# One-hot matrices for two pairs of edge tiles by one comparison, with its row of numbers in PSUM, in a graph network on one Trainium2 core

## The chip, the core and the metric

The kernel runs on one of the eight cores of a Trainium2 chip. A core has five engines that work side by side and wait for each other through semaphores: TensorE (PE in the profile, its weight loads PEld), VectorE (DVE), ScalarE (ACT), GpSimd (POOL) and SyncE (SP). SBUF is the working memory, 128 partitions wide; PSUM, in eight banks of 2 KB per partition, takes TensorE's results. The metric is the time of one execution in microseconds (us), as the device counts it; the median of three runs is compared.

## The reference

There are 6250 nodes with 256 features and 100000 edges, sorted by their destination, with 32 attributes and one of three types each. Three layers follow each other, and then the input is added and each node normalised:

```python
ew = edge_attr @ edge_w + edge_b
inv_cnt = [1.0 / max(segment_sum(type == i, dst), 1.0) for i in range(3)]
for l in range(3):
    msg = relu(x[src] * ew)
    out = zeros((n, 256))
    for i in range(3):
        h = segment_sum(msg * (type == i), dst) * inv_cnt[i]
        out = out + h @ weights[l, i]
    x = x + relu(out + x @ roots[l] + biases[l])
return layernorm(x_in + x)
```

All is fp32.

## The kernel before

The edges are cut into tiles of 128, two of which make a pair: 391 pairs, taken in a fixed order (`order`). Two pairs form a block `q`. A step (`it`) of the loop in `layer` stands for one pair, and code for pairs that lie ahead is issued in it, so that each engine's instructions stand in the order in which the loop writes them (`tc.manual_schedule`); nothing reorders them. Per step and in this order the loop

- gathers the source rows of the pair nine steps ahead, by two indirect DMAs from GpSimd (`gather_pair`, L1054) into a row tile `xs` for two pairs, of which there are eight (`rows`, `bufs=ROWS`); in the first layer from the input, later from `x_mid`, which the layer before wrote. The first three row tiles of the whole run lie in `x_root` instead;
- reduces the pair itself (`reduce`, L687 or L695): a matmul of its messages with the one-hot matrix of each of its tiles, 120 columns for 3 types x 40 nodes, summed over a span of pairs in a bank of `h_p`;
- multiplies edge attributes by `edge_w` for the pair five ahead (`make_ew`, L634), into `ew_p`, which ScalarE has filled with the bias (L621);
- weighs the block three ahead (`weigh`): VectorE multiplies `xs` by `ew_p` in place (L656), ScalarE takes the relu (L657);
- handles one root chunk of 128 nodes, about every six steps: `root_turn` transposes `x_all` on TensorE (L728), two steps later ScalarE copies that (L732), at the third step TensorE multiplies by `roots` (L736), and at the sixth VectorE adds the bias and keeps it in `x_root` (`root_keep`, L739);
- handles a node chunk whose edges are all in: TensorE multiplies the sums in `acc` by `weights` (`node_mul`, L754), VectorE scales and adds them to `x_root` (L785), adds the relu to `x_all` (L788), and SyncE writes the rows to `x_mid` (L791), or in the last layer VectorE normalises them (L806) and SyncE writes the output;
- builds the one-hot matrices of the block two ahead (`one_hot`, L669): four comparisons on VectorE, one for each tile, of the numbers 0 to 119 (`iota_w`, in SBUF) with the number `seg` of each edge. In the first layer ScalarE makes a bf16 copy (L673), from which edges are counted;
- adds a finished span's sums from `h_p` into the ring `acc` (`add`, L723).

At the start of layers 1 and 2 the first six pairs are gathered before the last node chunk is written; `complete` adds what that chunk brings, by matmuls (L649) and an add (L651).

PSUM is full: `ew_p` has four banks, `h_p` two, `o_p` and `r_p` one each. A tile of `r_p` holds a root chunk's transposes in its first half and its product in the second. `complete` and `node_mul` take turns between `o_p` and `r_p`: the second pair of a block in `complete`, and the second part of node chunks 0 and 1, go to `r_p`. Chunks 1 and 0 are the last two of a layer.

Of the kernel before, what the change touches and what calls it, by code (L numbers as in the profile page):

```python
# [8 lines left out]
F32 = mybir.dt.float32  # L9
BF = mybir.dt.bfloat16  # L10
I32 = mybir.dt.int32
AF = mybir.ActivationFunctionType
ALU = mybir.AluOpType
# [429 lines left out]
def ordered_path(ctx, tc, x, attr_laid, A, weights, roots, biases, edge_w, edge_b, out, src, src_i, seg, place_i, consts, x_root,  # L443
# [6 lines left out]
    nc = tc.nc  # L450
    P = 128
    N, D = x.shape
    E = src.shape[0]
    L, R = weights.shape[:2]
# [5 lines left out]
    DC = D // P  # L460
    WK = R * WIN
# [11 lines left out]
    ident, ones, iota_w = consts  # L473
# [14 lines left out]
    with tc.tile_pool(name="bias_s", bufs=1) as bias_s:  # L488
# [5 lines left out]
        part = bias_s.tile([P, D], BF, name="part")  # L494
# [10 lines left out]
    x_all = big.tile([P, NT, D], F32, name="x_all")  # L505
# [28 lines left out]
    wpool = ctx.enter_context(tc.tile_pool(name="wpool", bufs=1))  # L534
    o_pool = ctx.enter_context(tc.tile_pool(name="o_p", bufs=1, space=PSUM))
    r_pool = ctx.enter_context(tc.tile_pool(name="r_p", bufs=1, space=PSUM))

    at_groups = list(dict.fromkeys(u // GROUP for u in order))

# [47 lines left out]
    def layer(l, r_sb, b_sb, ats, early, pools):  # L587
# [11 lines left out]
        xs, ew_ps, ohs, h_ps, h_ss, o_ps, rs = {}, {}, {}, {}, {}, {}, {}  # L599
        x0s, mvs, oh_bs, t_ss, places = {}, {}, {}, {}, []  # L600
# [12 lines left out]
        def pairs_of(q):  # L613
            return range(min(2, U - 2 * q))
# [29 lines left out]
        def complete(q):  # L644
            for k in pairs_of(q):

                rest = (r_pool if k else o_pool).tile([P, 2, D], F32, name="r_p" if k else "o_p")
                for i in range(2):
                    nc.tensor.matmul(rest[:, i, :], came[:, 4 * q + 2 * k + i - 2 * order[0], :], x_all[:, 0, :],  # L649
                                     start=True, stop=True)  # L650
                nc.vector.tensor_add(xs[q][:, k], rest, xs[q][:, k])  # L651
# [13 lines left out]
        def one_hot(q):  # L665
            ohs[q] = edge.tile([P, 4, WK], F32, name="oh", bufs=3)
            n = 2 * len(pairs_of(q))
            for t in reversed(range(n)):
                nc.vector.tensor_scalar(ohs[q][:, t, :].rearrange("p (r w) -> p r w", r=R), iota_w[:, :, :WIN], seg[:, 4 * q + t:4 * q + t + 1], None,  # L669
                                        op0=ALU.is_equal)  # L670
            if l == 0:
                oh_bs[q] = edge.tile([P, 4, WK], BF, name="oh_b", bufs=3)
                nc.scalar.activation(oh_bs[q][:, :n], ohs[q][:, :n], AF.Copy)  # L673
# [49 lines left out]
            nc.vector.tensor_tensor(there, h_ps[span][:, :CH * WK].rearrange("p (c r w) -> p c r w", c=CH, r=R), there, op=ALU.add)  # L723

        def root_turn(c):
            rs[c] = r_pool.tile([P, 2, DC * P], F32, name="r_p")
            for d in range(DC):
                nc.tensor.transpose(rs[c][:, 0, d * P:(d + 1) * P], x_all[:, c, d * P:(d + 1) * P], ident)  # L728

        def root_turned(c):  # L730
            t_ss[c] = edge.tile([P, DC, P], F32, name="t_s", bufs=1)
            nc.scalar.activation(t_ss[c], rs[c][:, 0, :], AF.Copy)  # L732

        def root_mul(c):
            for d in range(DC):
                nc.tensor.matmul(rs[c][:, 1, :], t_ss[c][:, d, :], r_sb[:, d, :], start=(d == 0), stop=(d == DC - 1))  # L736

        def root_keep(c):
            nc.vector.tensor_add(x_root[:, at_root[c], :], rs[c][:, 1, :], b_sb)  # L739
            if l == L - 1:  # L740
                nc.vector.tensor_add(x_all[:, c, :], x_all[:, c, :], x0s[c])

        def parts_of(c):
            return ((0,), (1, 2)) if c else ((0,), (1,), (2,))

        def node_mul(c, part):

            n = min(P, N - c * P)
            slot = slot_of(c)
            o_p = o_ps[c, part] = (r_pool if part == 1 and c < 2 else o_pool).tile(  # L750
                [P, 2, D], F32, name="r_p" if part == 1 and c < 2 else "o_p")
            for j, r in enumerate(parts_of(c)[part]):
                for d in range(DC):
                    nc.tensor.matmul(o_p[:n, j, :], acc[:, d, r, slot:slot + n], w_sb[:, r * DC + d, :],  # L754
                                     start=(d == 0), stop=(d == DC - 1))
            if l == 0 and part == 0:
                for r in range(R):
                    nc.tensor.transpose(o_p[:n, 1, r:r + 1], acc[0:1, DC, r, slot:slot + n], ident[0:1, 0:1])

        def slot_of(c):  # L760
            return c % (RING // P) * P if c > 1 else ASIDE + c * P
# [57 lines left out]
        at_root = {c: (j + 2 * FIRST) % ROOTS for j, c in enumerate(turns_of)}  # L819
# [8 lines left out]
        for it in range(-11, max(starts) + 8):  # L828
            def pair(k):
                return order[it + k] if 0 <= it + k < U else None  # L830
# [28 lines left out]
            if pair(3) is not None and first_of(it + 3, 2):  # L859
                if l > 0 and it + 3 < FIRST:  # L860
                    complete(pair(3) // 2)
                if pair(3) // 2 != order[-1] // 2:
                    weigh(pair(3) // 2)

            if pair(3) is not None and pair(3) // 2 == order[-1] // 2:
                k = pair(3) % 2
# [6 lines left out]
            if it - 6 in root_at:  # L873
                root_keep(root_at[it - 6])
            if it in root_at:
                root_turn(root_at[it])
            if it - 2 in root_at:
                root_turned(root_at[it - 2])
            if it - 3 in root_at:
                root_mul(root_at[it - 3])  # L880
# [13 lines left out]
            if it in node_at:  # L894
                node_mul(node_at[it], 0)
            if it - 2 in node_at:
                node_mul(node_at[it - 2], 1)
                if node_at[it - 2] == 0:
                    node_mul(0, 2)
# [4 lines left out]
            if pair(2) is not None and first_of(it + 2, 2) and pair(2) // 2 != order[-1] // 2:  # L904
                one_hot(pair(2) // 2)
            if pair(3) is not None and first_of(it + 3, 2) and pair(3) // 2 == order[-1] // 2:
                one_hot(pair(3) // 2)
# [14 lines left out]
WIN = 40  # L922
# [137 lines left out]
def kernel(ctx, tc, x, src, dst, edge_attr, edge_type, weights, roots, biases, edge_w,  # L1060
# [110 lines left out]
    with tc.If(unordered == 0):  # L1171
        ordered_path(tc, x, attr_laid, edge_attr.shape[1], weights, roots, biases, edge_w, edge_b, out, src, src_i, seg, place_i,
                     (ident, ones, iota_w), x_root, first_rows, node_i)
# [51 lines left out]
```

## Time and profile before

| | us |
|---|---|
| median of three runs | 2961.4 (2960.73 to 2961.57) |
| the profiled execution | 2962.46 |
| its span, first to last instruction | 2960.2 |
| GpSimd busy / idle before its gathers | 2228.8 / 715.8 |
| VectorE busy | 1998.2 |
| four comparisons of a block, all 2346 | 622.9 |

The profile page gives for each engine the time in which it was busy with instructions, groups of instructions by line with the mean duration of one and the idle time before them, and the waits with what ended them. [...] Timeline rows read: start, duration, engine, line, operation, output <- inputs with partitions x elements, count, and in brackets the idle time before and what released it. Rows by windows give a stretch, its length, then for each engine the busy time and the number of instructions.

### The profile page before, as it was taken

To read this page: it belongs to the slowest core of one execution; us is meant where nothing else is said; L and a number is where in the kernel's file an instruction comes from. 1 tells how busy PE (TensorE), PEld (TensorE's weight loads), DVE (VectorE), ACT (ScalarE), POOL (GpSimd) and SP (SyncE) were. 2 spreads that over 40 slices of the span, in tenths; PEclk is the share of its full clock that TensorE was granted. 3 is DMA by queue.
4 is the path that set the end of the run, shared out by engine and by line. 5 is a ranking of instruction groups with operands and counts; after the bars stand their busy time and mean duration, and the time that the engine had idled before them with its cause. 6 is when DMAs were issued, how large, how long until landed. Compare 5 with 4: busy or idle time off the path is not lost. (4 is left out here: it accounts for less than half of the span.)

```text
span 2960.2 us, 43407 instructions
## 1 busy us (share of the span) xinstructions
PE 2591.9 (88%) x13712; PEld 1782.6 (60%) x13712; DVE 1998.2 (68%) x4910; ACT 1503.8 (51%) x1911; POOL 2228.8 (75%) x2355
## 2 busy tenths in 40 slices
PE   5999999999998878888889998778888888999876
PEld 2666677677765545556666666454555666666644
DVE  6666677778775555566767776545666777888864
ACT  4666656556565444454444444435444444444443
POOL 7777777777777777777777777777777777777776
PEclk9999999999999999999999999889999999999998
DMA  5444444444444444444444444444444444444443
GB/s 168 151 143 136 148 124 125 127 130 130 127 134 128 132 116 120 129 122 124 127 125 130 130 132 129 136 132 125 126 133 133 135 133 132 139 137 137 129 125 97
DMA packets 173705, 387.39 MB, mean 131 GB/s; under 512 B 43594, under 2 KB 79068, under 8 KB 173468
## 3 DMA queue, kind: packets, MB, share of 16 engines
q0 software_dynamic: 112608, 307.65, 36.4%
q1 hardware_dynamic: 53280, 68.50, 7.2%
q10 hardware_dynamic: 7580, 8.37, 1.0%
q8 instruction: 113, 1.85, 0.3%
q14 instruction: 124, 1.02, 0.1%
HBM read 364.89 MB, written 19.46 MB: 130 GB/s over the span
## 5 line engine op out<-in xcount | busy, mean ns | idle before, releaser
L1054 POOL DMA_INDIRECT xs<-x_mid,src_r x1540 | 1460.5, 948 | 469.1 <-issue 363.4
L657 ACT ACTIVATE xs<-xs 128x1024 f32<-128x1024 f32 (+1 forms) x585 | 615.7, 1053 | 1301.0 <-DVE xs L656 1296.5
L656 DVE TENSOR_TENSOR xs<-ew_p,xs 128x1024 f32<-128x1024 f32 (+1 forms) x585 | 711.4, 1216 | 676.7 <-DMA xs<-x_mid,src_r 429.8
L1054 POOL DMA_INDIRECT xs<-in_x_dram,src_io x770 | 732.0, 951 | 234.6 <-issue 192.3
L695 PEld LDWEIGHTS h_p<-oh,xs 128*128 128x128 f32 x5160 | 669.7, 196 | 251.9 <-issue 123.8
L695 PE MATMUL h_p<-oh,xs 128*128 128x120 f32 x5160 | 734.3, 287 | 86.4 <-issue 34.5
L634 PE MATMUL ew_p<-ew_sb,at 64*128 64x512 f32 x2346 | 687.6, 662 | 95.8 <-ACT ew_p L621 92.3
L669 DVE TENSOR_SCALAR oh<-iota_w,seg_o 128x120 f32<-128x120 f32 x2346 | 622.9, 327 | 0.0
L687 PE MATMUL h_p<-xs,oh 128*120 128x256 f32 x2088 | 570.9, 407 | 22.9 <-issue 7.8
L621 ACT ACTIVATE ew_p<-seed 128x1024 f32<-128x1024 f32 x582 | 588.9, 1012 | 0.0
L754 PE MATMUL o_p<-w_sb,acc 128*128 128x256 f32 (+1 forms) x1728 | 440.7, 391 | 28.2 <-DVE x_root L785 24.2
L687 PEld LDWEIGHTS h_p<-xs,oh 128*120 128x120 f32 x2088 | 363.1, 191 | 162.8 <-issue 48.1
L723 DVE TENSOR_TENSOR acc<-h_p,acc 128x240 f32 (+1 forms) x732 | 323.7, 442 | 173.2 <-PE o_p L754 69.6
L754 PEld LDWEIGHTS o_p<-w_sb,acc 128*128 128x128 f32 (+1 forms) x1728 | 309.3, 191 | 152.0 <-DVE x_root L785 62.7
L634 PEld LDWEIGHTS ew_p<-ew_sb,at 64*128 64x128 f32 x2346 | 181.9, 189 | 224.9 <-ACT ew_p L621 121.1
L785 DVE SCALAR_TENSOR_TENSOR x_root<-o_p,inv,x_root 128x256 f32<-128x256 f32 (+1 forms) x432 | 207.0, 479 | 28.3 <-PE o_p L754 21.6
L736 PE MATMUL r_p<-r_sb,t_s 128*128 128x256 f32 x588 | 160.1, 395 | 26.1 <-ACT t_s L732 25.8
L771 ACT ACTIVATE acc<-zero_o 128x768 f32<-128x768 f32 (+1 forms) x150 | 140.2, 934 | 15.3 <-PE o_p L754 14.7
L673 ACT ACTIVATE oh_b<-oh 128x480 bf16<-128x480 f32 x196 | 116.3, 594 | 56.1 <-DVE oh L669 55.2
L728 PEld LDWEIGHTS r_p<-ident_o,x_all 128*128 128x128 f32 x294 | 30.9, 144 | 169.0 <-DVE x_root L739 116.7
L736 PEld LDWEIGHTS r_p<-r_sb,t_s 128*128 128x128 f32 x588 | 103.0, 192 | 47.6 <-ACT t_s L732 36.4
L728 PE MATMUL r_p<-ident_o,x_all 128*128 128x128 f32 x294 | 65.4, 305 | 69.3 <-DVE x_root L739 69.1
(110 smaller groups left out, 940.8 us busy)
## 6 DMA issues: line engine op xcount, KB each, us to landing
at<-in_attr_laid_dram SPq DMA_DIRECT2D x147, 256.0 KB
xs<-x_mid,src_r POOLq DMA_INDIRECT x1540, 2.8
xs<-in_x_dram,src_io POOLq DMA_INDIRECT x770, 2.8
x_mid<-x_all SPq DMA_DIRECT2D x96, 128.0 KB
x_all<-in_x_dram ACTq DMA_DIRECT2D x8, 768.0 KB
x<-in_x_dram SPq DMA_DIRECT2D x48, 128.0 KB
out_dram<-x_all SPq DMA_DIRECT2D x48, 128.0 KB
w_sb<-in_L_gnn_weights_dram SPq DMA_DIRECT2D x3, 768.0 KB
```

What stands on the lines that cost most here:

```text
L621: nc.scalar.activation(ew_ps[q][:, :n], seed[:, None, :, :].to_broadcast([P, n, 2, D]), AF.Copy)
L634: nc.tensor.matmul(ew_ps[q][:, k].rearrange("p i d -> p (i d)"), at[half, :], ew_sb[half].rearrange("p i d -> p (i d)"), start=False, stop ...
L656: nc.vector.tensor_mul(there, ew_ps[q][:, pairs.start:pairs.stop], there)
L657: nc.scalar.activation(there, there, AF.Relu)
L669: nc.vector.tensor_scalar(ohs[q][:, t, :].rearrange("p (r w) -> p r w", r=R), iota_w[:, :, :WIN], seg[:, 4 * q + t:4 * q + t + 1], None, o ...
L687: nc.tensor.matmul(h_p[:WK, :D], ohs[u // 2][:, t, :], xs[u // 2][:, u % 2, i, :], start=(i == 0 and first), stop=(i == 1 and closes(u)), ...
L695: nc.tensor.matmul(h_p[:, d * WK:(d + 1) * WK], xs[u // 2][:, u % 2, i, d * P:(d + 1) * P] if d < DC else full_ones, (ohs if d < DC else o ...
L723: nc.vector.tensor_tensor(there, h_ps[span][:, :CH * WK].rearrange("p (c r w) -> p c r w", c=CH, r=R), there, op=ALU.add)
L736: nc.tensor.matmul(rs[c][:, 1, :], t_ss[c][:, d, :], r_sb[:, d, :], start=(d == 0), stop=(d == DC - 1))
L754: nc.tensor.matmul(o_p[:n, j, :], acc[:, d, r, slot:slot + n], w_sb[:, r * DC + d, :], start=(d == 0), stop=(d == DC - 1))
L785: nc.vector.scalar_tensor_tensor(root, o_p[:n, j, :], inv[:n, c, r:r + 1], root, op0=ALU.mult, op1=ALU.add)
L1054: nc.gpsimd.indirect_dma_start(out=xs[:, u % 2, i, :], out_offset=None, in_=x_rows[:, :], in_offset=bass.IndirectOffsetOnAxis(ap=src_i[:, ...
```

## The change

One bank of `r_p` is held by one tile for the whole run. Its second half takes a copy of the numbers 0 to 119, written once (L539 of the changed kernel). The first half serves a root chunk's transposes and then, over them, its product. `one_hot` becomes one `tensor_tensor` per block (L671): the row of numbers from PSUM, repeated for each tile, against `seg`, repeated over 120 columns. `complete` uses `o_p` for both its pairs, and of the node chunks only chunk 0's second part still uses `r_p`'s half bank.

```diff
--- before.py
+++ after.py
@@ -534,6 +534,9 @@
     wpool = ctx.enter_context(tc.tile_pool(name="wpool", bufs=1))
     o_pool = ctx.enter_context(tc.tile_pool(name="o_p", bufs=1, space=PSUM))
     r_pool = ctx.enter_context(tc.tile_pool(name="r_p", bufs=1, space=PSUM))
+    r_bank = r_pool.tile([P, 4 * P], F32, name="r_p")
+    r_p, places_p = r_bank[:, :D], r_bank[:, None, D:D + WK]
+    nc.vector.tensor_copy(r_bank[:, D:D + WK].rearrange("p (r w) -> p r w", r=R), iota_w[:, :, :WIN])
 
     at_groups = list(dict.fromkeys(u // GROUP for u in order))
 
@@ -644,7 +647,7 @@
         def complete(q):
             for k in pairs_of(q):
 
-                rest = (r_pool if k else o_pool).tile([P, 2, D], F32, name="r_p" if k else "o_p")
+                rest = o_pool.tile([P, 2, D], F32, name="o_p")
                 for i in range(2):
                     nc.tensor.matmul(rest[:, i, :], came[:, 4 * q + 2 * k + i - 2 * order[0], :], x_all[:, 0, :],
                                      start=True, stop=True)
@@ -665,9 +668,8 @@
         def one_hot(q):
             ohs[q] = edge.tile([P, 4, WK], F32, name="oh", bufs=3)
             n = 2 * len(pairs_of(q))
-            for t in reversed(range(n)):
-                nc.vector.tensor_scalar(ohs[q][:, t, :].rearrange("p (r w) -> p r w", r=R), iota_w[:, :, :WIN], seg[:, 4 * q + t:4 * q + t + 1], None,
-                                        op0=ALU.is_equal)
+            nc.vector.tensor_tensor(ohs[q][:, :n], places_p.to_broadcast([P, n, WK]),
+                                    seg[:, 4 * q:4 * q + n, None].to_broadcast([P, n, WK]), op=ALU.is_equal)
             if l == 0:
                 oh_bs[q] = edge.tile([P, 4, WK], BF, name="oh_b", bufs=3)
                 nc.scalar.activation(oh_bs[q][:, :n], ohs[q][:, :n], AF.Copy)
@@ -723,20 +725,19 @@
             nc.vector.tensor_tensor(there, h_ps[span][:, :CH * WK].rearrange("p (c r w) -> p c r w", c=CH, r=R), there, op=ALU.add)
 
         def root_turn(c):
-            rs[c] = r_pool.tile([P, 2, DC * P], F32, name="r_p")
             for d in range(DC):
-                nc.tensor.transpose(rs[c][:, 0, d * P:(d + 1) * P], x_all[:, c, d * P:(d + 1) * P], ident)
+                nc.tensor.transpose(r_p[:, d * P:(d + 1) * P], x_all[:, c, d * P:(d + 1) * P], ident)
 
         def root_turned(c):
             t_ss[c] = edge.tile([P, DC, P], F32, name="t_s", bufs=1)
-            nc.scalar.activation(t_ss[c], rs[c][:, 0, :], AF.Copy)
+            nc.scalar.activation(t_ss[c].rearrange("p d e -> p (d e)"), r_p, AF.Copy)
 
         def root_mul(c):
             for d in range(DC):
-                nc.tensor.matmul(rs[c][:, 1, :], t_ss[c][:, d, :], r_sb[:, d, :], start=(d == 0), stop=(d == DC - 1))
+                nc.tensor.matmul(r_p, t_ss[c][:, d, :], r_sb[:, d, :], start=(d == 0), stop=(d == DC - 1))
 
         def root_keep(c):
-            nc.vector.tensor_add(x_root[:, at_root[c], :], rs[c][:, 1, :], b_sb)
+            nc.vector.tensor_add(x_root[:, at_root[c], :], r_p, b_sb)
             if l == L - 1:
                 nc.vector.tensor_add(x_all[:, c, :], x_all[:, c, :], x0s[c])
 
@@ -747,8 +748,7 @@
 
             n = min(P, N - c * P)
             slot = slot_of(c)
-            o_p = o_ps[c, part] = (r_pool if part == 1 and c < 2 else o_pool).tile(
-                [P, 2, D], F32, name="r_p" if part == 1 and c < 2 else "o_p")
+            o_p = o_ps[c, part] = r_p[:, None, :] if part == 1 and c == 0 else o_pool.tile([P, 2, D], F32, name="o_p")
             for j, r in enumerate(parts_of(c)[part]):
                 for d in range(DC):
                     nc.tensor.matmul(o_p[:n, j, :], acc[:, d, r, slot:slot + n], w_sb[:, r * DC + d, :],
```

The program puts waits between engines that use one bank. Three places show it; the names in brackets are semaphores, PE_49 of TensorE, DVE_49 of VectorE, Activation_49 of ScalarE, DMASW of gathers. VectorE in layer 1, from a `root_keep` to the adds into `acc`, before:

```order
L739 TENSOR_TENSOR x_root<-r_p,b_sb 128x256
L669 TENSOR_SCALAR oh<-iota_w,seg_o 128x120 x4
L656 TENSOR_TENSOR xs<-ew_p,xs 128x1024 [waits DMASW1_49,DMASW6_49,DMASW0_49,DMASW7_49,PE_49,Activation_49]
L785 SCALAR_TENSOR_TENSOR x_root<-o_p,inv,x_root 128x256 [waits PE_49]
L669 TENSOR_SCALAR oh<-iota_w,seg_o 128x120 x4
L716 TENSOR_LOAD place_i
L723 ISA
L723 TENSOR_TENSOR acc<-h_p,acc 128x6x40 [waits DVE_49,PE_49,Activation_49]
```

The same place in the change (lines are three higher here, those of `one_hot` and `root_keep` two and one):

```order
L740 TENSOR_TENSOR x_root<-r_p,b_sb 128x256
L671 TENSOR_TENSOR oh<-r_p,seg_o 128x480 [waits PE_49]
L659 TENSOR_TENSOR xs<-ew_p,xs 128x1024 [waits DMASW6_49,DMASW1_49,DMASW7_49,DMASW0_49,Activation_49]
L785 SCALAR_TENSOR_TENSOR x_root<-o_p,inv,x_root 128x256 [waits PE_49]
L671 TENSOR_TENSOR oh<-r_p,seg_o 128x480 [waits PE_49]
L718 TENSOR_LOAD place_i
L725 ISA
L725 TENSOR_TENSOR acc<-h_p,acc 128x6x40 [waits DVE_49,Activation_49]
```

Each four comparisons are one, and it waits for TensorE: the first for the transposes of the step's `root_turn`, the second for the product of `root_mul`. Over the whole program 137 of the 588 comparisons wait for a `root_turn` and 147 for a `root_mul`; before, none did.

TensorE in `complete` at the start of layer 1, before:

```order
L649 MATMUL o_p<-x_all,came 128x256 [waits DVE_49]
L649 MATMUL o_p<-x_all,came 128x256
L649 MATMUL r_p<-x_all,came 128x256 x2
L634 MATMUL ew_p<-ew_sb,at 128x512 [waits DVE_49,Activation_49]
L634 MATMUL ew_p<-ew_sb,at 128x512
L649 MATMUL o_p<-x_all,came 128x256 [waits PE_49]
L649 MATMUL o_p<-x_all,came 128x256
L649 MATMUL r_p<-x_all,came 128x256 [waits PE_49]
L649 MATMUL r_p<-x_all,came 128x256
```

And in the change:

```order
L652 MATMUL o_p<-x_all,came 128x256 [waits DVE_49]
L652 MATMUL o_p<-x_all,came 128x256
L652 MATMUL o_p<-x_all,came 128x256 [waits DVE_49]
L652 MATMUL o_p<-x_all,came 128x256
L637 MATMUL ew_p<-ew_sb,at 128x512 [waits DVE_49,Activation_49]
L637 MATMUL ew_p<-ew_sb,at 128x512
L652 MATMUL o_p<-x_all,came 128x256 [waits PE_49]
L652 MATMUL o_p<-x_all,came 128x256
L652 MATMUL o_p<-x_all,came 128x256 [waits DVE_49]
L652 MATMUL o_p<-x_all,came 128x256
```

The second pair's matmuls now go to `o_p` and wait for VectorE, which must have added the first pair.

TensorE at node chunk 1 in layer 0, second part, before:

```order
L687 MATMUL h_p<-xs,oh 120x256 [waits DMASW1_49]
L690 LDWEIGHTS oh_b
L690 MATMUL h_p<-full_ones,oh_b 120x1
L634 MATMUL ew_p<-ew_sb,at 128x512 [waits DVE_49,Activation_49]
L634 MATMUL ew_p<-ew_sb,at 128x512
L754 MATMUL r_p<-w_sb,acc 128x256 x4
L687 MATMUL h_p<-xs,oh 120x256 [waits DMASW2_49,DVE_49]
```

And in the change:

```order
L689 MATMUL h_p<-xs,oh 120x256 [waits DMASW1_49]
L692 LDWEIGHTS oh_b
L692 MATMUL h_p<-full_ones,oh_b 120x1
L637 MATMUL ew_p<-ew_sb,at 128x512 [waits DVE_49,Activation_49]
L637 MATMUL ew_p<-ew_sb,at 128x512
L754 MATMUL o_p<-w_sb,acc 128x256 [waits DVE_49,PE_49]
L754 MATMUL o_p<-w_sb,acc 128x256 x3
L689 MATMUL h_p<-xs,oh 120x256 [waits DMASW2_49]
```

The second part (two types) goes to the bank of the first and waits until VectorE has used that; what follows is the reduction of the next pair. GpSimd's and SyncE's instructions and their waits stay in the same order.

## The prediction

> **What bounds the kernel now.** I read the page's busy shares and groups first, then the timeline of GpSimd, the waits, and the counts of finished work at a few moments.
>
> ```profile
> span 2960.2 us, 43407 instructions
> PE 2591.9 (88%) x13712; PEld 1782.6 (60%) x13712; DVE 1998.2 (68%) x4910; ACT 1503.8 (51%) x1911; POOL 2228.8 (75%) x2355
> L1054 POOL DMA_INDIRECT xs<-x_mid,src_r x1540 | 1460.5, 948 | 469.1 <-issue 363.4
> L1054 POOL DMA_INDIRECT xs<-in_x_dram,src_io x770 | 732.0, 951 | 234.6 <-issue 192.3
> ```
>
> TensorE shows 88% and GpSimd only 75%, so the page seems to name TensorE. The timeline says otherwise:
>
> ```profile
> 1502.65 0.94 POOL L1054 DMA_INDIRECT xs<-x_mid,src_r  x1 [0.30 <-issue]
> 1503.22 1.22 DVE L656 TENSOR_TENSOR xs<-ew_p,xs 128x1024 f32<-128x1024 f32 x1 [2.11 <-PE h_p L695]
> 1503.90 0.94 POOL L1054 DMA_INDIRECT xs<-x_mid,src_r  x1 [0.30 <-issue]
> 1504.67 1.06 DVE L669 TENSOR_SCALAR oh<-iota_w,seg_o 128x120 f32<-128x120 f32 x4
> 1505.15 0.95 POOL L1054 DMA_INDIRECT xs<-x_mid,src_r  x1 [0.30 <-PE o_p L754]
> ...
> POOL xs L1054 <- issue: 562.1, 1845, 0.3
> DVE xs L656 <- DMA xs<-x_mid,src_r: 429.8, 236, 5.1
> DVE xs L656 <- DMA xs<-in_x_dram,src_io: 112.1, 67, 5.3
> ...
> 2944.28 0.95 POOL L1054 DMA_INDIRECT xs<-x_mid,src_r  x1 [0.30 <-issue]
> ```
>
> A gather starts every 1.25 us: 0.95 busy and 0.30 before the next, always 0.30, whoever is named as releaser. The two large groups make 2310 gathers; busy 2192.5 plus idle 703.7 is 2896.2 us, 1.254 us each. The 36 gathers that are left, by the same 1.254, make 45 us, together 2941, and the last one starts at 2944.28. So GpSimd issues gathers from start to end and never waits for a buffer. VectorE, on the other hand, stands 541.9 us before the weighing (L656) until gathered rows have landed. The kernel is bound by the number of gathers times 1.25 us, plus 16 us behind the last of them.
>
> **The change part by part.** Its sum is made against the profiled execution: span 2960.2, its own time 2962.46, so 2.3 lie around the span; the median of the runs is 2961.4, or 1.1 less.
>
> *Gathers.* The order of GpSimd's gathers and what each waits for stay as they are. Only their pace could move, by what VectorE does meanwhile:
>
> ```profile
> L1054 POOL DMA_INDIRECT xs<-x_mid,src_r x128 | 121.1, 946 | 39.0 <-issue 27.7 <-ACT ew_p L621 2.7 <-PE h_p L695 2.7
> ...
> 871.62 0.43 DVE L788 SCALAR_TENSOR_TENSOR x_all<-x_root,x_all 128x256 f32<-128x256 f32 x1
> 871.67 1.19 POOL L1054 DMA_INDIRECT xs<-in_x_dram,src_io  x1 [0.30 <-issue]
> ...
> L788 DVE SCALAR_TENSOR_TENSOR x_all<-x_root,x_all 128x256 f32<-128x256 f32 x144 | 61.4, 427 | 5.0
> L806 DVE TENSOR_SCALAR x_all<-x_all,mv 128x256 f32<-128x256 f32 x48 | 21.6, 450 | 1.8
> L741 DVE TENSOR_TENSOR x_all<-x_all,x 128x256 f32<-128x256 f32 x49 | 20.3, 415 | 0.0
> ```
>
> The first row is the group between 1500 and 1660 us: an undisturbed gather takes 946 ns. Over the whole run the means are 948 and 951, so all disturbances together cost 1460.5 + 732.0 - 2310 x 0.946 = 7.2 us. The disturbed gather at 871.67 took 1.19 us because L788, whose two tensors both lie in SBUF, ran over its start. L656, with one tensor in PSUM and one in SBUF, ran over the start of the gather at 1503.90, which took 0.94; the old comparisons ran over the one at 1505.15, which took 0.95. The new comparison (L671) has L656's placing: numbers in PSUM, `seg` in SBUF. I take 0 for it. Lower bound: -7.2 us, if every disturbance vanished. Upper bound: if it disturbed as L788, L806 and L741 do, which is the first rival.
>
> *VectorE.* Removed are 2346 comparisons, added are 588.
>
> ```profile
> L669 DVE TENSOR_SCALAR oh<-iota_w,seg_o 128x120 f32<-128x120 f32 x2346 | 622.9, 327 | 0.0
> L723 DVE TENSOR_TENSOR acc<-h_p,acc 128x360 f32 x243 | 128.0, 527 | 103.8 <-ACT oh_b L673 26.1 <-PE o_p L754 23.8 <-PE h_p L709 22.2
> L656 DVE TENSOR_TENSOR xs<-ew_p,xs 128x512 f32<-128x512 f32 x6 | 4.1, 686 | 0.6 <-DMA xs<-x_mid,src_r 0.3 <-ACT xs L657 0.2
> ```
>
> Four old ones take 1.06 us (the 1504.67 row). A new one has 480 elements from PSUM and SBUF; between 360 (527 ns) and 512 (686 ns) the slope is 159 / 152 = 1.046 ns, so 480 take 686 - 32 x 1.046 = 653 ns, with 527 and 686 as ends. VectorE is spared 622.9 - 588 x 0.653 = 239 us. On the path that sets the end this is 0: VectorE already waits for gathers, and will wait 239 us more. The one copy that fills the row (L539) adds 0.2 to 0.5 us ahead of the first layer (L1127 copies one number in 132 ns, L499 casts 256 in 434 ns). What covers it there:
>
> ```profile
> L499 DVE CAST part<-left 128x256 bf16<-128x256 f32 x3 | 1.3, 434 | 4.0 <-DMA left<-in_L_gnn_edge_b_dram 4.0
> L1127 DVE COPY base_g<-base 1x1 f32<-1x1 f32 x32 | 2.0, 132 | 0.0
> 0.00:57.30 57.30, 9.11 (x32) 4.61 (x32) 1.00 0.63 182
> 59.69 0.95 POOL L1054 DMA_INDIRECT xs<-in_x_dram,src_io  x1 [0.30 <-issue]
> ```
>
> At 57.3 us 32 matmul records of L687, or eight pairs, are done; with them the first row tile of the ring is free, and the first gather that needs it starts at 59.69. That is 2.4 us of cover, the least anywhere.
>
> [...]
>
> *The bank's waits.* Root transposes, root products and the row of numbers now share a bank, and the program puts waits between them: 137 of the 588 comparisons wait for TensorE's root transposes, 147 for its root products. Queued behind a waiting comparison on VectorE are the adds into `acc` (TensorE waits for those to reuse `h_p`), the node updates and the next weighing. A root chunk comes about every 6 steps, 15 us. TensorE does the product right behind the first pair's reduction of the same step, so a comparison may stand until that is done; it is needed only two steps, 5 us, later. I take 0 on the path: what hides it is the distance between gathering and reducing.
>
> ```profile
> 0.00:600.00 600.00, 451.80 (x475) 0.99 0.48 140
> 0.00:600.00 600.00, 110.60 (x899) 99.43 (x900) 0.99 0.48 140
> 0.00:600.00 600.00, 164.96 (x564) 85.64 (x564) 0.99 0.48 140
> 0.00:825.00 825.00, 621.99 (x654) 0.99 0.47 137
> 0.00:825.00 825.00, 164.96 (x564) 85.64 (x564) 0.99 0.47 137
> 0.00:825.00 825.00, 217.57 (x1760) 194.68 (x1761) 0.99 0.47 137
> ```
>
> These are counts up to 600 and 825 us, in two orders: at 600 gathers (L1054), then the matmul records of the reductions, L695 and L687; at 825 gathers, L687, L695. A pair of tiles is 2 gathers and either 4 records of L687 (141 pairs at both moments) or 10 of L695. At 600 us 141 + 90 = 231 pairs are reduced, 462 gathers' worth of 475; at 825 us 141 + 176 = 317, so 634 of 654. The ring of eight row tiles holds 32. TensorE, VectorE and the rest thus lag by 13 to 20 gathers. A tile is free when both its pairs are reduced, so at 825 us 158 tiles and 8 more allow 664 gathers, and 10 of them, 12.5 us, would have to be lost before GpSimd stops. From 600 to 825 us they lose 7 gathers: this is the only long stretch in which they, not the gathers, set their own pace, and there VectorE has 0.4 us less per comparison.
>
> *One bank fewer for the rest.* `complete` has its two pairs in one bank, so TensorE's second pair waits for the first add:
>
> ```profile
> L651 DVE TENSOR_TENSOR xs<-o_p,xs 128x512 f32<-128x512 f32 x6 | 4.1, 692 | 23.0 <-PE o_p L649 23.0
> 1000.00:1020.00 20.00, 12.37 (x45) 8.01 (x46) 11.13 (x24) 7.00 (x8) 15.13 (x17) 0.91 0.48 136
> ```
>
> That is 3 x 0.7 = 2 us at the start of layers 1 and 2. The second row (TensorE, its weight loads, VectorE, ScalarE, GpSimd) shows 7.6 us of TensorE idle in the 20 us that follow in layer 1, which take it up. Node chunk 1 now waits for its first part's update, as every chunk from 2 on does already; it comes 38 steps ahead of the layer's end. Chunk 0 keeps both its banks. All this: 0 on the path, 2 us if the cover were gone.
>
> *Behind the last gather.*
>
> ```profile
> 2944.76 3.95 PE L695 MATMUL h_p<-oh,xs 128*128 128x120 f32 x32 [1.06 <-ACT xs L657]
> 2945.43 1.06 DVE L669 TENSOR_SCALAR oh<-iota_w,seg_o 128x120 f32<-128x120 f32 x4
> 2947.08 0.42 DVE L662 TENSOR_TENSOR xs<-ew_p,xs 128x256 f32<-128x256 f32 x1 [0.25 <-DMA xs<-x_mid,src_r]
> 2948.75 0.41 DVE L723 TENSOR_TENSOR acc<-h_p,acc 128x240 f32<-128x240 f32 x1 [1.25 <-PE h_p L695]
> ```
>
> The last comparison is 0.4 us shorter, but the last weighing waits for the last gather's landing (0.25 us of DMA wait), and TensorE is busy all the while. 0.
>
> Sum: 0 + 0 + 0 + 0 + 0, so 2960.2 + 2.3 = 2962.5 for a run like the profiled one, and 2961.4 for the median. What a measurement of this kernel can tell from no change is taken as 0.2%, 5.9 us.
>
> **The rivals.**
>
> *The comparison disturbs the gathers* (slower, the other side). For: the gather at 871.67 shows that VectorE can hold one up. Price: the three groups above have 103 us and cost at most 7.2, or 7%; 588 x 0.653 = 384 us at 7% are 27 us, 2988. It decides from 1.5% on (5.9 of 384). Against: L656 alone has 711 us in PSUM and SBUF; at 7% it would cost 50 us, and 7.2 is all there is. [...] By that rule I give this rival 5 in 100; the 0.94 beside L656 agrees.
>
> *The shared bank makes the reductions fall behind* (slower). If each comparison in the 52 blocks of 5 us between 600 and 860 us cost TensorE 0.5 us, 26 us would be lost; 12.5 are covered, GpSimd stops for 13.5, 2975. It decides from (12.5 + 5.9) / 52 = 0.35 us per block on. For: TensorE is nearly full there, and each lost 1.25 us is a gather. Against: only one block in three has a root product. 8 in 100.
>
> *Fewer disturbances* (faster). Other times of VectorE move L788 and its like off the gathers' starts: up to 7.2 us less, 2954; 5 in 100 that it is more than 5.9. The opposite, as many again meeting the gathers' starts (2969), gets 3.
>
> [...]
>
> **How the numbers follow.** No change 79 in 100 (the comparison that is not shorter among it); disturbed gathers 5, falling behind 8, more meetings 3, which makes slower 16; faster 5. Range: down to 2955, where most disturbances are gone; up to 2970, which takes in most of the second rival and an equal number of disturbances again (2961.4 + 7.2). Within the forecast alone it would be 2957 to 2966.
>
> **What would show it.** In the profile of the change: gathers still 0.30 us apart from start to end, mean 946 to 951 ns; L671 588 times at about 650 ns; VectorE's busy time about 240 us less and its wait for landings at L656 longer by as much; new waits of L671 for `r_p` without a GpSimd wait behind them. Wrong it would be if GpSimd showed a wait over 0.3 us, or gathers under L671 took over 946 ns.

## The result and the profile after

The changed kernel takes 2988.6 us (median of 4 runs, 2987.1 to 2989.7), the kernel before 2961.5: 1.0091 times as long, interval 1.0073 to 1.0108. It is slower by 27 us, outside the forecast range (2955 to 2970) and on the side that had 16 chances in 100.

The page of the changed kernel, beside the rows of before in the prediction:

```profile
span 2985.5 us, 41294 instructions
PE 2589.1 (87%) x13712; PEld 1771.5 (59%) x13712; DVE 1761.7 (59%) x3153; ACT 1503.6 (50%) x1911; POOL 2227.8 (75%) x2355
L1054 POOL DMA_INDIRECT xs<-x_mid,src_r x1540 | 1459.6, 948 | 469.1 <-issue 389.3
L1054 POOL DMA_INDIRECT xs<-in_x_dram,src_io x770 | 732.1, 951 | 260.3 <-issue 220.0
L671 DVE TENSOR_TENSOR oh<-r_p,seg_o 128x480 f32<-128x480 f32 x588 | 382.2, 650 | 532.8 <-PE r_p L737 417.9
```

VectorE works 236.5 us less, and a comparison takes 650 ns. Gathers are as long as before, 948 and 951 ns. The idle time of GpSimd ahead of the gathers of layers 1 and 2 is unchanged to the tenth (469.1), but in layer 0 it has grown from 234.6 to 260.3: 25.7 us, nearly the whole loss. And L671 now stands 532.8 us in waits, most of it for the root products (L737). The group of gathers between 500 and 900 us, before and after (count, busy time and mean ns, idle time before them):

```profile
L1054 POOL DMA_INDIRECT xs<-in_x_dram,src_io x319 | 303.2, 951 | 97.2 <-issue 79.8 <-PE h_p L695 4.3 <-ACT ew_p L621 3.4
```

```profile
L1054 POOL DMA_INDIRECT xs<-in_x_dram,src_io x299 | 284.6, 952 | 116.8 <-issue 100.5 <-ACT xs L660 4.6 <-ACT ew_p L624 2.7
```

With 0.304 us before each, 319 gathers have 97.0 us of idle time: there was no wait before. 299 have 90.9, so 25.9 us of real waiting have come in, all of it in this stretch.

The waits between 570 and 850 us, first of before, then of after (us in total, times, longest):

```profile
POOL xs L1054 <- issue: 55.2, 181, 0.3
PE h_p L695 <- DVE acc L723: 8.3, 12, 1.3
PE h_p L695 <- issue: 0.2, 1, 0.2
```

```profile
POOL xs L1054 <- issue: 73.7, 180, 2.8
DVE oh L671 <- PE r_p L737: 54.4, 15, 5.0
PE h_p L697 <- issue: 14.5, 12, 1.2
DVE oh L671 <- PE r_p L729: 10.4, 10, 1.8
PE h_p L697 <- DVE acc L725: 7.4, 11, 1.2
```

Fifteen comparisons stood 3.6 us each for a root product. TensorE stood 8.5 us ahead of the reductions before (L695) and stands 21.9 us there now (L697): what is put down to the adds is about the same, and 14.3 us more, in twelve pieces, have no releaser named. One of them, from the timeline of the changed kernel (start, duration):

```profile
685.69 0.94 POOL L1054 DMA_INDIRECT xs<-in_x_dram,src_io  x1 [0.90 <-issue]
...
687.11 1.08 PE L737 MATMUL r_p<-r_sb,t_s 128*128 128x256 f32 x4
...
688.23 0.66 DVE L671 TENSOR_TENSOR oh<-r_p,seg_o 128x480 f32<-128x480 f32 x1 [1.67 <-PE r_p L737]
688.81 0.53 DVE L725 TENSOR_TENSOR acc<-h_p,acc 128x360 f32 x1
...
689.25 1.22 DVE L659 TENSOR_TENSOR xs<-ew_p,xs 128x1024 f32<-128x1024 f32 x1
...
689.43 0.68 PE L697 MATMUL h_p<-oh,xs 128*128 128x120 f32 x4 [1.24 <-issue]
```

TensorE ends the root product at 688.19. Only then does VectorE compare (0.66 us), and only behind that comes the add of finished sums (L725), which ends at 689.34. 0.09 us later TensorE starts the next reduction: 1.24 us in which it had nothing to do. L725 gives TensorE its bank of sums back, and it was queued behind a comparison that waited for TensorE. The profile writes "issue" here, so that the add is what TensorE needed is read here from the times alone; the experiment with the add in front tests it.

What this does to the distance between gathering and reducing is seen in the counts up to 380, 600 and 825 us (gathers L1054; records of L697, 10 to a pair; of L689, 4 to a pair; three views):

```profile
0.00:380.00 380.00, 284.98 (x300) 0.99 0.50 148
0.00:600.00 600.00, 450.93 (x475) 0.99 0.48 139
0.00:825.00 825.00, 604.27 (x636) 1.00 0.46 133
```

```profile
0.00:600.00 600.00, 102.74 (x827) 90.67 (x828) 0.99 0.48 139
0.00:825.00 825.00, 202.13 (x1630) 178.89 (x1630) 1.00 0.46 133
```

```profile
0.00:380.00 380.00, 163.49 (x561) 83.60 (x562) 0.99 0.50 148
0.00:600.00 600.00, 164.58 (x564) 84.04 (x564) 0.99 0.48 139
```

At 600 us 141 + 82.7 pairs are reduced, 447 gathers' worth of 475: a lag of 28 where it was 13. The ring of 32 is used up, since a tile comes free only with both its pairs. From there to 825 us GpSimd starts only 161 gathers instead of 179, at the pace of the reductions: 80.3 pairs in 225 us, 5.60 us for a block of two, against 86 pairs and 5.23 us before and 5.0 us that four gathers take.

### The profile page after: what moved, and what is told of

Same layout as the page of the kernel before. It is cut to its first block, busy times and chain, and to the rows that moved or that the text cites. A ratio compares the mean times of both kernels' runs of the same rounds, so it can differ in the third digit from the quotient of the medians.

```text
span 2985.5 us, 41294 instructions
## 1 busy us (share of the span) xinstructions
PE 2589.1 (87%) x13712; PEld 1771.5 (59%) x13712; DVE 1761.7 (59%) x3153; ACT 1503.6 (50%) x1911; POOL 2227.8 (75%) x2355
## 5 line engine op out<-in xcount | busy, mean ns | idle before, releaser
L1054 POOL DMA_INDIRECT xs<-x_mid,src_r x1540 | 1459.6, 948 | 469.1 <-issue 389.3
L1054 POOL DMA_INDIRECT xs<-in_x_dram,src_io x770 | 732.1, 951 | 260.3 <-issue 220.0
L697 PEld LDWEIGHTS h_p<-oh,xs 128*128 128x128 f32 x5160 | 663.1, 195 | 292.5 <-issue 188.3
L697 PE MATMUL h_p<-oh,xs 128*128 128x120 f32 x5160 | 730.7, 287 | 121.7 <-issue 79.2
L671 DVE TENSOR_TENSOR oh<-r_p,seg_o 128x480 f32<-128x480 f32 x588 | 382.2, 650 | 532.8 <-PE r_p L737 417.9
L689 PE MATMUL h_p<-xs,oh 128*120 128x256 f32 x2088 | 570.3, 406 | 54.1 <-issue 41.1
L689 PEld LDWEIGHTS h_p<-xs,oh 128*120 128x120 f32 x2088 | 360.0, 190 | 202.5 <-issue 97.3
L754 PE MATMUL o_p<-w_sb,acc 128*128 128x256 f32 (+1 forms) x1752 | 447.7, 392 | 28.3 <-DVE x_root L785 25.4
L725 DVE TENSOR_TENSOR acc<-h_p,acc 128x240 f32 (+1 forms) x732 | 324.4, 443 | 137.9 <-PE o_p L754 74.1
L737 PE MATMUL r_p<-r_sb,t_s 128*128 128x256 f32 x588 | 157.8, 391 | 21.0 <-ACT t_s L733 21.0
L737 PEld LDWEIGHTS r_p<-r_sb,t_s 128*128 128x128 f32 x588 | 102.5, 190 | 40.0 <-ACT t_s L733 28.7
L729 PEld LDWEIGHTS r_p<-ident_o,x_all 128*128 128x128 f32 x294 | 31.0, 142 | 123.1 <-DVE x_root L740 59.5
L697 PE MATMUL h_p<-oh_b,full_ones 128*128 128x120 bf16 x430 | 93.3, 217 | 0.0
```

Source lines behind the costliest of these rows:

```text
L671: nc.vector.tensor_tensor(ohs[q][:, :n], places_p.to_broadcast([P, n, WK]), seg[:, 4 * q:4 * q + n, None].to_broadcast([P, n, WK]), op=ALU ...
L689: nc.tensor.matmul(h_p[:WK, :D], ohs[u // 2][:, t, :], xs[u // 2][:, u % 2, i, :], start=(i == 0 and first), stop=(i == 1 and closes(u)), ...
L697: nc.tensor.matmul(h_p[:, d * WK:(d + 1) * WK], xs[u // 2][:, u % 2, i, d * P:(d + 1) * P] if d < DC else full_ones, (ohs if d < DC else o ...
L737: nc.tensor.matmul(r_p, t_ss[c][:, d, :], r_sb[:, d, :], start=(d == 0), stop=(d == DC - 1))
L1054: nc.gpsimd.indirect_dma_start(out=xs[:, u % 2, i, :], out_offset=None, in_=x_rows[:, :], in_offset=bass.IndirectOffsetOnAxis(ap=src_i[:, ...
```

## The experiments

Theories: *bank* (the comparison waits for TensorE's root work because the row lies in that bank; what is queued behind it makes TensorE late, and in layer 0 the lag uses up the ring); *merge* (one comparison for two pairs is itself what hurts); *disturbance* (the comparison holds gathers up). Each ratio compares with the kernel before, run anew beside it: 2962.0 us for the row in SBUF, the four comparisons, the comparison in front and the change in layers 1 and 2 only, 2961.5 us for the others.

**The row in SBUF.** The change with its row of numbers elsewhere; nothing else differs.

```diff
-    r_p, places_p = r_bank[:, :D], r_bank[:, None, D:D + WK]
+    row = big.tile([P, 1, WK], F32, name="row")
+    r_p, places_p = r_bank[:, :D], row
-    nc.vector.tensor_copy(r_bank[:, D:D + WK].rearrange("p (r w) -> p r w", r=R), iota_w[:, :, :WIN])
+    nc.vector.tensor_copy(row[:, 0, :].rearrange("p (r w) -> p r w", r=R), iota_w[:, :, :WIN])
```

> The changed kernel with its row of numbers in SBUF instead of the bank of root products; the one comparison of 480 elements, the bank's layout and the order of all instructions stay. Bank theory (the comparison waits for the root product that TensorE does in the same step, the adds queued behind it are held, and TensorE loses time in layer 0): L671's waits for r_p (54 us between 570 and 850 us) are gone, GpSimd shows no gap over 0.4 us between 500 and 900 us, and the time is 2961 plus whatever a comparison with both inputs in SBUF does to gathers. Disturbance theory (VectorE with all operands in SBUF holds gathers up as L788 does, 7% of its time): 588 x 0.65 x 7% = 27 us, seen as a gather mean of about 958 ns instead of 948 ns all over the run, and again about 2988 by another way. Merge theory (one comparison for two pairs is itself what is late): gaps of GpSimd as in the changed kernel, 2988.

It took 3015.1 us, 1.0179 times before (1.0163 to 1.0194). Page, then TensorE's wait ahead of the reductions from 570 to 850 us:

```profile
L1055 POOL DMA_INDIRECT xs<-x_mid,src_r x1540 | 1496.0, 971 | 469.1 <-issue 363.4
L1055 POOL DMA_INDIRECT xs<-in_x_dram,src_io x770 | 748.1, 972 | 234.6 <-issue 194.4
L672 DVE TENSOR_TENSOR oh<-row,seg_o 128x480 f32<-128x480 f32 x588 | 380.7, 647 | 0.0
```

```profile
PE h_p L698 <- DVE acc L726: 9.1, 13, 1.2
```

Both halves of the expectation came true at once. The comparison waits for nothing (0.0), and GpSimd's idle time is back at 234.6 and 469.1, the figures of before. The slower gathers of this run leave the reductions more time, so these figures alone don't clear the merging; but TensorE, too, waits as before ahead of the reductions (9.1 us against 8.5, none of it without a releaser). One comparison for two pairs is not what hurts, the merge theory is out. But gathers now take 971 and 972 ns. Over 946 ns that is 1496.0 + 748.1 - 2185.3 = 58.8 us, 51.6 more than the 7.2 of before, and nearly the whole of the 53 us that it is slower. That is 13.6% of the comparison's 381 us, twice the 7% that I had put on it. The trace says where it falls: 275 of the 588 comparisons run while a gather starts, and these 275 gathers take 53.1 us over 946 ns in sum; all the others together take 6.5. One such gather from the timeline:

```profile
745.69 0.65 DVE L672 TENSOR_TENSOR oh<-row,seg_o 128x480 f32<-128x480 f32 x1
745.75 1.41 POOL L1055 DMA_INDIRECT xs<-in_x_dram,src_io  x1 [0.30 <-issue]
```

So the place in PSUM does avoid this loss, all of it: with the row in PSUM gathers are 6.4 us over 946 ns in sum (1459.6 + 732.1 - 2185.3), no more than before, and the 284 gathers that start while a comparison runs take 946 ns on average.

**Four comparisons that read the bank.** The waits without the merging:

```diff
-            nc.vector.tensor_tensor(ohs[q][:, :n], places_p.to_broadcast([P, n, WK]),
-                                    seg[:, 4 * q:4 * q + n, None].to_broadcast([P, n, WK]), op=ALU.is_equal)
+            for t in reversed(range(n)):
+                nc.vector.tensor_scalar(ohs[q][:, t, :], places_p[:, 0, :], seg[:, 4 * q + t:4 * q + t + 1], None,
+                                        op0=ALU.is_equal)
```

> The four comparisons of before, but reading the row of numbers from the bank of root products: the waits of the change without the merging. Bank theory: the same waits and more work behind them (four comparisons take 0.4 us more than the one), so 2988 or more, up to 3010. Merge theory: as before, 2961.

3022.7 us, 1.0208 (1.0192 to 1.0223): 13 us beyond the upper end of what I expected, but on the bank theory's side. Page, then the gathers from 300 to 500 and from 500 to 900 us:

```profile
L672 DVE TENSOR_SCALAR oh<-r_p,seg_o 128x120 f32<-128x120 f32 x2346 | 637.7, 334 | 563.8 <-PE r_p L738 425.8
```

```profile
L1055 POOL DMA_INDIRECT xs<-in_x_dram,src_io x151 | 143.5, 950 | 57.8 <-issue 50.5 <-ACT h_s L706 1.2 <-PE h_p L693 0.9
L1055 POOL DMA_INDIRECT xs<-in_x_dram,src_io x282 | 266.9, 946 | 133.9 <-issue 112.9 <-ACT xs L660 6.9 <-ACT ew_p L624 3.7
```

About the same waits (563.8 us against 532.8), with 1.34 us of comparing behind each instead of 0.65. GpSimd waits 57.8 - 151 x 0.304 = 11.9 us in the first stretch and 133.9 - 282 x 0.304 = 48.2 us in the second, 60 in all, and it starts to wait ahead of 500 us. The waits alone, added to the comparisons of before, make the kernel slower; the merging made their price smaller.

**The comparison in front.** The change, with `one_hot` called ahead of `root_keep` in the step instead of behind `node_mul`, so ahead of that step's root and node work:

```diff
+            if pair(2) is not None and first_of(it + 2, 2) and pair(2) // 2 != order[-1] // 2:
+                one_hot(pair(2) // 2)
+            if pair(3) is not None and first_of(it + 3, 2) and pair(3) // 2 == order[-1] // 2:
+                one_hot(pair(3) // 2)
             if it - 6 in root_at:
                 root_keep(root_at[it - 6])
...
-            if pair(2) is not None and first_of(it + 2, 2) and pair(2) // 2 != order[-1] // 2:
-                one_hot(pair(2) // 2)
-            if pair(3) is not None and first_of(it + 3, 2) and pair(3) // 2 == order[-1] // 2:
-                one_hot(pair(3) // 2)
```

> The changed kernel, with the comparison written ahead of the root and node work of its step instead of behind it. It then waits for the root product of an earlier step, not of its own. Bank theory: waits for r_p at L671 shrink to under a third of 54 us between 570 and 850 us, GpSimd's gaps there (24 us in the changed kernel) are under 5 us, 2961 to 2966. Merge theory: 2988.

2966.7 us, 1.0019 (1.0010 to 1.0028), 0.7 us above what I expected. Waits of the comparison from 570 to 850 us, and gathers from 500 to 900 us:

```profile
DVE oh L671 <- PE r_p L729: 21.6, 12, 3.4
DVE oh L671 <- ACT t_s L733: 8.1, 11, 1.0
DVE oh L671 <- PE r_p L737: 0.4, 1, 0.4
```

```profile
L1054 POOL DMA_INDIRECT xs<-in_x_dram,src_io x318 | 301.2, 947 | 100.7 <-issue 81.8 <-PE h_p L697 5.2 <-ACT ew_p L624 3.9
L1054 POOL DMA_INDIRECT xs<-in_x_dram,src_io x770 | 730.7, 949 | 240.1 <-issue 194.8
```

The wait for the root products is gone, but that for the transposes (L729) has doubled, from 10.4 to 21.6 us: all waits for `r_p` together fall from 64.8 to 22.0 us, which is more than the third of 54 us that I expected. GpSimd waits 100.7 - 96.7 = 4.0 us there instead of 25.9, and 22 of the 27 us are back. In all of layer 0 (second row) it waits 5.5 us more than before, which is the rest; 1.5 of them fall at 60 and 97 us, near the start of the run. Whether the waits for the transposes that are left cause it was not tried.

**The add in front.** The change, with the finished sums added before the comparison; the comparison keeps its place behind the root product:

```diff
+            for span in add_at.get(it, ()):
+                add(span)
             if pair(2) is not None and first_of(it + 2, 2) and pair(2) // 2 != order[-1] // 2:
                 one_hot(pair(2) // 2)
...
-            for span in add_at.get(it, ()):
-                add(span)
```

> The changed kernel with the add of a finished span's sums (L725 in the changed kernel) written ahead of the comparison instead of behind it; the comparison waits for the root product as in the change. If TensorE loses its time because the adds queued behind the waiting comparison are late (it needs the bank of sums back), the time falls to 2962 to 2972 although the comparison still waits over 40 us between 570 and 850 us. If what is late is the weighing behind the comparison, or the matrices themselves, it stays at 2980 to 2990.

2965.6 us, 1.0014 (1.0005 to 1.0024). The same two views, with TensorE's waits beside the comparison's:

```profile
DVE oh L671 <- PE r_p L737: 40.4, 12, 4.4
PE h_p L697 <- issue: 5.9, 3, 2.1
```

```profile
L1054 POOL DMA_INDIRECT xs<-in_x_dram,src_io x318 | 302.2, 950 | 98.1 <-issue 85.4 <-ACT ew_p L624 2.7 <-DMA xs<-in_x_dram,src_io 1.2
L1054 POOL DMA_INDIRECT xs<-x_mid,src_r x1540 | 1464.3, 951 | 469.5 <-issue 376.2
L1054 POOL DMA_INDIRECT xs<-in_x_dram,src_io x770 | 732.8, 952 | 235.9 <-issue 198.8
```

The comparison still waits 40 us, but TensorE's 14.5 us without a releaser are down to 5.9, and GpSimd waits 98.1 - 96.7 = 1.4 us. So the late matrices and the late weighing are not what stops GpSimd: it is the add queued behind the wait, for which TensorE waits in turn. The wait is not free even so, as the reductions' records up to 600 and 825 us show:

```profile
0.00:600.00 600.00, 108.18 (x890) 98.41 (x890) 0.99 0.48 140
0.00:825.00 825.00, 210.33 (x1720) 190.26 (x1720) 0.99 0.47 137
```

At 600 us the reductions are as far as before (890 records against 899). From there to 825 us they do 83 pairs, 5.42 us for a block, against 5.60 in the change and 5.23 before: about half of what they lost there is still lost, and now the ring hides it. What is left of the loss in time lies elsewhere: the gathers (the two lower rows, whole run) are 1464.3 + 732.8 - 2185.3 = 11.8 us over 946 ns in this execution, 4.6 more than before.

**Ten row tiles** in the changed kernel (`ROWS = 10`).

> The changed kernel with ten row tiles instead of eight. If GpSimd stops only because the reductions have fallen behind by the whole ring, two more tiles are 8 more gathers of room, 8 x 1.25 = 10 us less: gaps of about 16 us instead of 25.7 us, 2978 to 2980. If GpSimd stops for another reason, 2988.

2978.2 us, 1.0056 (1.0041 to 1.0072).

```profile
L1054 POOL DMA_INDIRECT xs<-in_x_dram,src_io x308 | 292.5, 950 | 108.9 <-issue 91.6 <-ACT ew_p L624 3.6 <-ACT acc L771 2.8
```

10.4 us less than the changed kernel, and the wait falls from 25.9 to 108.9 - 93.6 = 15.3 us: 8 gathers' worth of room, as worked out.

**The change in layers 1 and 2 only**; layer 0 compares as before, from SBUF, while the bank's layout stays as changed:

```diff
-            nc.vector.tensor_tensor(ohs[q][:, :n], places_p.to_broadcast([P, n, WK]),
-                                    seg[:, 4 * q:4 * q + n, None].to_broadcast([P, n, WK]), op=ALU.is_equal)
+            if l == 0:
+                for t in reversed(range(n)):
+                    nc.vector.tensor_scalar(ohs[q][:, t, :].rearrange("p (r w) -> p r w", r=R), iota_w[:, :, :WIN], seg[:, 4 * q + t:4 * q + t + 1], None,
+                                            op0=ALU.is_equal)
+            else:
+                nc.vector.tensor_tensor(ohs[q][:, :n], places_p.to_broadcast([P, n, WK]),
+                                        seg[:, 4 * q:4 * q + n, None].to_broadcast([P, n, WK]), op=ALU.is_equal)
```

> The changed kernel, but layer 0 uses the four comparisons of before from SBUF; layers 1 and 2 keep the one comparison from PSUM. Theory that only layer 0 pays (there the reductions have the least room): 2961, with the waits of L671 for r_p in layers 1 and 2 (125 and 115 us in the changed kernel) still there and no GpSimd gap behind them. Theory that the comparison costs in all layers: about 2961 + 2/3 x 27 = 2979.

2962.4 us, 1.0002 (0.9992 to 1.0011): no difference. The comparison in layers 1 and 2 (L676) still waits for root work:

```profile
L676 DVE TENSOR_TENSOR oh<-r_p,seg_o 128x480 f32<-128x480 f32 x392 | 254.7, 650 | 278.7 <-PE r_p L742 236.0
L1059 POOL DMA_INDIRECT xs<-in_x_dram,src_io x770 | 731.8, 950 | 234.6 <-issue 192.6
```

279 us of waits cost nothing that shows where the reductions have time in hand, and since the layout is the changed one throughout, the one bank fewer in `complete` and for node chunk 1 costs nothing either.

**A sum left in PSUM.** A side step on the gathers: in the kernel before, the last scaled sum of a node chunk stays in its bank, so that the add into `x_all` (L788 there) has only one input in SBUF.

```diff
-                nc.vector.scalar_tensor_tensor(root, o_p[:n, j, :], inv[:n, c, r:r + 1], root, op0=ALU.mult, op1=ALU.add)
+                last = part == len(parts_of(c)) - 1 and j == len(parts_of(c)[part]) - 1
+                kept = o_p[:n, j, :] if last else root
+                nc.vector.scalar_tensor_tensor(kept, o_p[:n, j, :], inv[:n, c, r:r + 1], root, op0=ALU.mult, op1=ALU.add)
...
-            nc.vector.scalar_tensor_tensor(x_all[:n, c, :], root, 0.0, x_all[:n, c, :], op0=ALU.max, op1=ALU.add)
+            nc.vector.scalar_tensor_tensor(x_all[:n, c, :], kept, 0.0, x_all[:n, c, :], op0=ALU.max, op1=ALU.add)
```

> The kernel before, with the last scaled sum of a node chunk left in its PSUM bank instead of x_root, so that the add into x_all (L788) has one input in PSUM and one in SBUF. If only instructions with all operands in SBUF hold gathers up, the 19 gathers that L788 held up by 3.0 us in sum are undisturbed: gathers take 4 to 5 us over 946 ns each in sum instead of 7.7 us, 2958 to 2959. If the place of the operands does not matter: 2961 to 2962.

> The same edit in the kernel with four comparisons in layer 0 and one from PSUM in layers 1 and 2 (2962.4 us). If only the gathers' pace counts there, 2958 to 2960, as with the kernel before; if the waits of L671 that are left take part, 2962 or more.

2959.7 us, 0.9993 (0.9984 to 1.0002), and with the same edit in the kernel that has the change in layers 1 and 2 only 2958.3 us, 0.9988 (0.9979 to 0.9997). The gathers of the two:

```profile
L1056 POOL DMA_INDIRECT xs<-x_mid,src_r x1540 | 1459.0, 947 | 469.1 <-issue 370.4
L1056 POOL DMA_INDIRECT xs<-in_x_dram,src_io x770 | 730.1, 948 | 236.3 <-issue 195.3
```

```profile
L1061 POOL DMA_INDIRECT xs<-x_mid,src_r x1540 | 1459.1, 947 | 469.1 <-issue 381.4
L1061 POOL DMA_INDIRECT xs<-in_x_dram,src_io x770 | 728.7, 946 | 235.4 <-issue 191.0
```

Over 946 ns each they are 3.8 and 2.5 us instead of 7.2. The adds show it one by one: before, 37 gathers start while an L788 runs, and 19 of them are held up, by 3.0 us in sum; with the edit 42 gathers start while one runs, and none is held up. In time the first gain (0.7 us short of what I expected) is not clear of no change: GpSimd's idle time in layer 0 is 236.3 us instead of 234.6, which takes half of what the gathers save. The second, 3 us below before, is clear, if barely; it is the fastest version here, but the runs of the two overlap, so that its lead of 1.4 us over the first is not certain.

## Why the prediction was wrong

- *What bounds the kernel* held in every run: the time is the number of gathers times their pace plus what GpSimd waits. For each kernel the two lines of GpSimd account for the difference in time to within 3 us.
- *Gathers, 0*: right. The comparison from PSUM disturbs none that can be seen (6.4 us in sum against 7.2). The first rival's price (2988) happens to be the time measured, but its mechanism is absent: the time alone would have named the wrong one, the row of GpSimd's idle time names the right one. That price, 7% of the time of an instruction with both inputs in SBUF, was half of what this comparison costs (13.6%): with the row in SBUF 275 gathers started while a comparison ran and paid 53.1 us, each by how much of it was then still to come, and the comparison (647 ns) is longer than the instructions from which I took the 7% (415 to 450 ns). The 5 in 100 for this rival rest on a rule that no run shows; what the runs show is that 284 gathers started while a comparison from PSUM ran and took 946 ns on average.
- *VectorE, 0*: right in its sizes (650 ns for 653, 236.5 us spared for 239), and the spared time was worth nothing. The comparison that is not shorter, counted in the 79 in 100, is shown by no run: one from PSUM took 650 ns, the four of before 1.06 us.
- *The bank's waits, 0*: this is the step that failed. I named what stands behind a waiting comparison, the adds into `acc` among it and that TensorE waits for those, and then priced only the lateness of the matrices themselves ("it is needed only two steps, 5 us, later"). The add is needed at once: in the changed kernel the reduction starts 0.09 us after it. With the add in front 23 of the 27 us are gone.
- *The cover of 10 gathers*: the right quantity, read at the wrong kernel. I took it at 825 us of before, and took 600 to 860 us as the stretch where reductions set their own pace. Slowed down, they fall behind from 380 us on: between 380 and 600 us, where before they kept step with the gathers, they take 2 x 220 / (223.7 - 140.2) = 5.27 us for a block, against 2 x 220 / (231 - 142.2) = 4.95 before (pairs by the counts shown, and by those of before at 380 us, L687 and L695):

```profile
0.00:380.00 380.00, 164.96 (x564) 85.64 (x564) 0.98 0.50 148
```

```profile
0.00:380.00 380.00, 1.35 (x12) 1.50 (x13) 0.98 0.50 148
```

  The lag, 300 - 284 = 16 gathers before at 380 us, is 300 - 280 = 20 there and grows to 28. So the cover was gone by 600 us, and all that followed went to GpSimd's wait.
- *The second rival* (the shared bank makes the reductions fall behind) is what happened, by its mechanism, though it starts at 380 us and not at 600, at 27 us instead of 13.5, and with 8 chances in 100. Its decisive rate, 0.35 us for a block of 5 us, was passed: 5.60 - 5.23 = 0.37 us from 600 to 825 us, and 0.32 already before. What I held against it, that only one block in three has a root product, is right for the product and leaves out the transposes: between 570 and 850 us 25 of 51 comparisons waited, 15 for the product and 10 for the transposes.
- *One bank fewer, and the end*: 0 within the noise, as forecast (the change in layers 1 and 2 only).

No run here leaves the wait for the bank out, so whether it could be dropped is not shown.

## What to carry to other kernels

When a change puts a wait ahead of other instructions of an engine, price the wait by whoever needs the instructions behind it soonest, and not by who needs the waiting instruction; here one instruction moved ahead of the wait gave back 23 of 27 us. Slack that is measured in a kernel holds for the pace of that kernel: ask how fast the covered side runs when slowed, and over how long a stretch, before setting a loss against it. The row of numbers in PSUM spared the gathers what it cost them from SBUF (6.4 us over 946 ns in sum against 58.8), but the comparison then stood 532.8 us in waits, most of it for the root work in its bank.

## What the runs showed of the hardware

A comparison with both inputs in SBUF, 647 ns long, cost GpSimd's gathers 13.6% of its own time (51.6 of 381 us). Nearly all of it was paid by gathers that started while one ran (275 gathers, 53.1 us over 946 ns; the other 2071, 6.5 us), by what was then still to come: with less than 0.13 us of the comparison left (55 gathers) they took 0.95 us as always, with 0.28 us left 1.10, and the one that started 60 ns into the comparison at 745.69 us took 1.41. The same comparison with one input in PSUM was as long (650 ns) and cost the gathers nothing measurable (284 started while it ran, 946 ns on average). Nor did the four comparisons of before, with one tensor input in SBUF: 512 gathers started while one ran, and took 946 ns on average. Comparing 120 numbers of a row with one took 334 ns from PSUM against 327 ns from SBUF, so the place hardly mattered to VectorE itself.
